# Layer 0 of a four-layer graph kernel: the sigmoid of r is transposed, and multiplied by the transposed x' on its way out of PSUM

## The chip, the cores and the metric

One core of one Trainium2 chip. The metric is the device time of one execution in microseconds. The kernel before was run three times; its median is 3438.73 us.

## The reference

Four layers on x (64 graphs, 256 nodes, 256 features) with adjacency adj (64 x 256 x 256), each followed by a residual sum and a layer norm. Layer 0 is a recurrence over the 256 nodes, and the change is in it alone:

```python
def step(h, i):
    x = jnp.take(h_e, i, axis=1)
    row = jnp.take(norm_adjT, i, axis=1)
    x_par = jnp.einsum('bj,bjd->bd', row, h)
    iou = x @ W_ioux.T + b_ioux + x_par @ W_iouh.T + b_iouh
    r, z = jnp.split(iou, 2, axis=1)
    r, z = (jax.nn.sigmoid(r), jax.nn.sigmoid(z))
    hc = jnp.tanh(x @ W_coux.T + b_coux + x_par * r @ W_couh.T + b_couh)
    h_new = z * x_par + (1.0 - z) * hc
    h = jax.lax.dynamic_update_slice(h, h_new[:, None, :], (0, i, 0))
    return (h, None)
```

Layer 1 is a graph convolution, layer 2 masked attention with one head, layer 3 masked attention with eight heads. All of it is in fp32.

## The kernel before

The kernel first sums, for all graphs, what the nodes not yet updated give to each node's x' (the code's `xp`, the reference's `x_par`). Then `_recurrence` runs 256 unrolled steps n. All 64 graphs are worked on at once: a state tile is 128 x 128, the two halves of the 256 features standing one under the other in the partitions, 64 graphs each. After the recurrence `_layers` runs the other three layers, graph by graph.

The order within the steps is written out by hand: inside the loop a manual schedule is in force, so each engine runs its instructions in the order in which the Python loop issues them, and waits in that order. What must go from one step to the next is a chain:

- x' is transposed by TensorE (`flip`, L611) and copied out of PSUM by ScalarE (L613) as `xpT`.
- `h_part` (L604) multiplies the h weights by it, first for gate r, later for z. Their x products (`x_part`, L596) and the bias are already in PSUM. r and the candidate c share one PSUM tile `rc`.
- ScalarE takes the sigmoid of r in place (L827). VectorE multiplies it by x' as `rx` (L829). `rx` is transposed (L611) and copied (L613) as `rT`, and `h_part` multiplies the candidate's weights by it.
- ScalarE takes the tanh (L861); VectorE makes `zcc` = (1 - z) * c (L863) and the next x' (L866) from it and from `v` (L852), which holds z * x' (`zx`, L843) and what GpSimd made `ready` (L803).
- The new state is added up by VectorE (L645) and copied by ScalarE as `hs` (L647).

Round this chain stands work that the queues fit in:

- `push` (L629) is one VectorE instruction that adds the last state, times an adjacency column, to the sum of one later node. p = n mod 8 decides how many there are: 5 at p = 0, then 10, 9, 8, 7, 6, 6, 4. In the loop they stand in groups: the one that the next node needs; up to 3 before `rx`; 1 after it; up to 4 after `v`. One that does not fit is left to the next step. `push_far` (L662, L666) does up to four more nodes at once on GpSimd.
- Fillers on TensorE: sums over older states (`late`, L520) at p = 0 to 3, `early` products (L417) or those of the x side (L212) at p = 4 to 7, where there are any. The first filler of a step stands behind the transpose of x', the second behind the z products. At p = 0 the second is twice as long, and the transposes of four x tiles (`flip_x`, L577) stand where the first would be; at p = 4 four more of them end the step. Results of fillers are copied out by ScalarE (L255), one or two at a step's middle and one at its end.
- The next step's r and c start with a copy of their bias by ScalarE (L837), then two x products of 256 columns: one between the transpose of `rx` and the c products, one behind the c products.
- Once in some steps VectorE makes degree sums (L303) at a step's end. The late sums travel through DRAM between steps 3 and 5 (L500, L506), and GpSimd adds them after steps 5 and 6 (L875).

The lines of the middle of a step, as they were:

```python
            push(3)
            ...
            h_part(z, 2, xpT)
            ...  # the second filler
            nc.scalar.activation(r, r, AF.Sigmoid)
            rx = new("rx", n, 1)
            nc.vector.tensor_mul(rx, r, xp)
            ...  # 1 - z, z, and the bias of the next rc
            rT = flip(rx, "rT", n)
            push(1)
            zx = keep[:, 2, :]
            nc.vector.tensor_mul(zx, z, xp)
```

Of the kernel before, what the change touches and what calls it, by code (L numbers as in the profile page):

```python
# [9 lines left out]
F32 = mybir.dt.float32  # L10
BF16 = mybir.dt.bfloat16
AF = mybir.ActivationFunctionType
# [7 lines left out]
P = 128  # L20
# [50 lines left out]
def _recurrence(tc, ident, Hd, x, adj, W_ioux, b_ioux, W_iouh, b_iouh, W_coux, b_coux, W_couh, b_couh, wide, then):  # L71
# [19 lines left out]
    nc = tc.nc  # L91
# [12 lines left out]
    with ExitStack() as ctx:  # L104
# [480 lines left out]
        def bias_part(G, gates):  # L585
            for o in range(2):
                nc.tensor.matmul(
                    G[o * B:(o + 1) * B], ones3, bias3[:, o, gates], start=True, stop=False,
                    skip_group_check=True,
                )  # L590

        def x_part(G, n, kc, gates):
            a, u = divmod(n, U)
            h, i = divmod(u, U // 2)
            for o in range(2):
                nc.tensor.matmul(  # L596
                    G[o * B:(o + 1) * B], xqT[a, i // 2][:, i % 2, kc, h * B:(h + 1) * B],
                    WxT[:, kc, o, gates], start=False, stop=False, skip_group_check=True,
                )

        def h_part(G, g, hT):
            for kc in range(2):
                for o in range(2):
                    nc.tensor.matmul(  # L604
                        G[o * B:(o + 1) * B], hT[:, kc * B:(kc + 1) * B], WhT[:, kc, o, g],
                        start=False, stop=(kc == 1), skip_group_check=True,
                    )

        def flip(src, tag, n):
            pt = ps.tile([P, P], F32, tag="flip", name=f"{tag}_ps_{n}")  # L610
            nc.tensor.transpose(pt, src, ident)  # L611
            t = new(tag, n, 1)
            nc.scalar.copy(t, pt)  # L613
            return t

        def new(tag, n, bufs=2):
            return work.tile([P, P], F32, tag=tag, name=f"{tag}_{n}", bufs=bufs)

        def cell(j, m, count=1):

            a, u = divmod(m, U)
            k, i = divmod(m, T)
            return sums[a][:, u:u + count, :], tables[k]["S"][:, LAG + j - k * T, i:i + count]

        def push(count):
            for _ in range(min(count, len(pushes))):
                m, j = pushes.pop(0)
                acc, s = cell(j, m)
                nc.vector.scalar_tensor_tensor(  # L629
                    acc[:, 0, :], keep[:, j % 2, :], s, acc[:, 0, :], ALU.mult, ALU.add  # L630
                )
# [80 lines left out]
        ps = ctx.enter_context(tc.tile_pool(name="r_ps", bufs=1, space=bass.MemoryType.PSUM))  # L712
# [9 lines left out]
        rc = ps.tile([P, 2, P], F32, tag="rc", name="rc_0", bufs=2)  # L722
# [9 lines left out]
        xp = new("xp", 0)  # L732
# [8 lines left out]
        def fill(side, n):  # L741

            try:
                side.send(n)
                return True
            except StopIteration:
                return False

        def fill_early(n):
            nonlocal x_left  # L750
            if not early_fill(n):
                for _ in range(2 if p in (6, 7) else 1):
                    if x_left and not fill(x_left, n):
                        x_left = None

        ctx.enter_context(tc.manual_schedule())
        for now in range(N):
            n = now
            k, i = divmod(n, T)
            p = n % U  # L760
            last = n + 1 == N

            xpT = flip(xp, "xpT", n)
# [25 lines left out]
            r, c = rc[:, 0, :], rc[:, 1, :]  # L789
# [10 lines left out]
            if not last:  # L800
# [3 lines left out]
                    ready, sums[(n + 1) // U][:, (n + 1) % U, :],  # L804
                    dinv[:, n + 1:n + 2].to_broadcast([P, P]),
                )
            push(3)
            if far:
                push_far(n - 1, hs, far[0], len(far))
            if behind:  # L810
# [7 lines left out]
                    early_parts.clear()  # L818
            h_part(z, 2, xpT)

            if p < 4:
                for _ in range(2 if p == 0 else 1):
                    fill(late_side, n) if late_side else None
            else:
                fill_early(n)

            nc.scalar.activation(r, r, AF.Sigmoid)  # L827
            rx = new("rx", n, 1)
            nc.vector.tensor_mul(rx, r, xp)  # L829
            zc = new("zc", n, 1)  # L830
            nc.scalar.activation(zc, z, AF.Sigmoid, scale=-1.0)
            nc.scalar.activation(z, z, AF.Sigmoid)
            if not last:
                rc = ps.tile([P, 2, P], F32, tag="rc", name=f"rc_{n + 1}", bufs=2)
# [2 lines left out]
                    nc.scalar.copy(rc, bias_rc)  # L837
                else:
                    bias_part(rc, slice(0, 2))
            rT = flip(rx, "rT", n)  # L840
            push(1)
            zx = keep[:, 2, :]
            nc.vector.tensor_mul(zx, z, xp)  # L843
            if not last:
                x_part(rc, n + 1, 0, slice(0, 2))
            h_part(c, 1, rT)
            for _ in range(2 if p == 3 else 1):
                next_of(copies, n)
            if not last:
                Sd = tables[kk]["Sd"][:, ii:ii + 1]  # L850
                v = keep[:, 3, :]
                nc.vector.scalar_tensor_tensor(v, zx, Sd, ready, ALU.mult, ALU.add)  # L852
                push(4)
                x_part(rc, n + 1, 1, slice(0, 2))
                z = ps.tile([P, P], F32, tag="z", name=f"z_ps_{n + 1}")
                bias_part(z, 2)
                for kc in range(2):
                    x_part(z, n + 1, kc, 2)
# [5 lines left out]
            if not last:  # L864
                xp = new("xp", n + 1)
# [542 lines left out]
def kernel(ctx: ExitStack, tc: tile.TileContext, ins, out):  # L1408
# [14 lines left out]
    def load_layers(load):  # L1423
        weights.extend(
            _load_layers(nc, wide, load, ins["L1_gnn_W"], ins["L1_gnn_b"], l2, l3)
        )

    _recurrence(
        tc, ident, Hd, x, adj,
        *(ins["L0_gnn_" + n] for n in (  # L1430
# [44 lines left out]
```

## Time and profile before

| what | value |
|---|---|
| median of 3 runs | 3438.73 us (3435.99 to 3442.99) |
| profiled execution, its own time: the span on the page | 3437.6 us |
| recurrence in it, first xpT copy to the last steps | 140.7 to 1525 us |
| TensorE busy, whole span | 3227.2 us (94%) |
| VectorE busy, whole span | 2499.7 us (73%) |
| ScalarE busy, whole span | 1883.7 us (55%) |
| GpSimd busy, whole span | 1873.5 us (55%) |
| pushes (L629) | 1712, 344 ns each |

The page names no time around the span for this execution; its span is taken as its time. PE is TensorE, PEld its weight loads, DVE VectorE, ACT ScalarE, POOL GpSimd, SP the engine that issues most DMAs. A timeline row gives an instruction's start in us from the span's start, its length, engine, line, operation, output and inputs, shapes, how many were merged (a 128 x 256 fp32 product stands as several records), and in brackets how long the engine was idle before it and what ended that. Starts that follow closer than the lengths are instructions that overlap in an engine's pipeline.

### The profile page before, as it was taken

The page shows a single profiled execution, that of the slowest core. Times are in us where ns is not written, and L with a number is a line of the kernel's source. Part 1 is how long each engine was busy: PE and PEld are TensorE (multiplying, and loading weights), DVE is VectorE, ACT ScalarE, POOL GpSimd, SP SyncE. Part 2 cuts the span into 40 slices and gives each one's busy share as a digit, 9 for nine tenths or more (in the row PEclk, how much of TensorE's full clock was granted, in tenths as well). Part 3 has the DMA queues.
Part 4 walks back from the last instruction along what each step waited for, and adds up shares of the span by engine and source line. Part 5 has one row for each costly group of instructions (what it writes and reads, how often), then busy time and mean ns, then how long its engine had stood idle before and what let it go on. Part 6 is the DMA issues. An engine that isn't in the chain of part 4 may idle for free.

```text
span 3437.6 us, 80347 instructions
## 1 busy us (share of the span) xinstructions
PE 3227.2 (94%) x29350; PEld 2321.8 (68%) x29350; DVE 2499.7 (73%) x7061; ACT 1883.7 (55%) x5010; POOL 1873.5 (55%) x2165
## 2 busy tenths in 40 slices
PE   5699999999889998878999999999999999999997
PEld 3555555555455555547888888888888888888885
DVE  3377777766667777755888888888888887888775
ACT  0155555544445554535666666666666666666664
POOL 2376777766657777733444444444444444444443
PEclk8999999999999999988999999999999999999999
DMA  9856576788777575130111111111111111111100
GB/s 280 245 156 150 159 189 154 169 193 204 194 185 175 148 176 153 58 97 22 47 47 47 47 47 47 47 47 47 47 47 47 47 47 47 47 47 47 47 29 19
DMA packets 389348, 347.88 MB, mean 101 GB/s; under 512 B 107357, under 2 KB 355305, under 8 KB 383721
## 3 DMA queue, kind: packets, MB, share of 16 engines
q1 hardware_dynamic: 371256, 325.82, 35.4%
q10 hardware_dynamic: 17696, 16.91, 1.5%
q8 instruction: 234, 3.83, 0.5%
q14 instruction: 162, 1.32, 0.1%
HBM read 224.01 MB, written 99.61 MB: 94 GB/s over the span
## 4 chain that ended last, share of the span: by engine, by line
PE 73%; DMA 7%; DVE 7%; POOL 4%; issue 3%; ACT 3%; SPq 2%; ACTq 0%; DVEq 0%; POOLq 0%
PE mm L996 13%; PE rc L604 5%; PE s L1180 4%; PE rc L596 4%; PE mm_2f L996 3%; PE mm_3v L996 3%; PE mm_t L996 3%; PE mm_3f L996 3%; PE mm_2v L996 3%; PE mm_g L996 3%; PE mm_2s L996 3%; PE mm_2w L996 3%; PE o L1215 3%; PE late L520 3%; DVE ACC L629 3%
## 5 line engine op out<-in xcount | busy, mean ns | idle before, releaser
L629 DVE SCALAR_TENSOR_TENSOR ACC<-keep,S,ACC 128x128 f32<-128x128 f32 x1712 | 504.0, 344 | 186.4 <-ACT hs L647 171.5
L1192 POOL TENSOR_TENSOR p3s<-p 128x256 f32<-128x256 f32 x512 | 387.2, 788 | 369.1 <-ACT p L1190 369.0
L996 PE MATMUL mm<-xT,weights 128*128 128x256 f32 x2048 | 483.9, 385 | 3.2 <-ACT xT L1078 3.2
L996 PEld LDWEIGHTS mm<-xT,weights 128*128 128x128 f32 x2048 | 386.4, 191 | 80.6 <-issue 25.5
L1189 DVE TENSOR_TENSOR p<-s,neg 128x512 f32<-128x512 f32 x512 | 317.5, 682 | 118.2 <-PE s L1180 118.2
L666 POOL TENSOR_TENSOR ACC<-ACC,far 128x384 f32<-128x384 f32 (+1 forms) x313 | 372.7, 1191 | 24.5
L596 PE MATMUL rc<-WxT,xqT 128*64 128x256 f32 x2048 | 324.6, 396 | 3.7 <-ACT rc L837 1.2
L662 POOL TENSOR_TENSOR far<-hs,S 128x384 f32<-128x384 f32 (+1 forms) x313 | 304.9, 974 | 4.7
L960 ACT ACTIVATE y<-y,shift,rstd 128x256 f32<-128x256 f32 x512 | 273.4, 599 | 47.4 <-DVE shift L958 43.4
L1190 ACT ACTIVATE p<-p 128x512 f32<-128x512 f32 x512 | 295.2, 628 | 2.1 <-DVE p L1189 1.6
L803 POOL TENSOR_TENSOR ready<-ACC,dinv 128x128 f32<-128x128 f32 x255 | 102.3, 401 | 335.3 <-DVE ACC L629 335.2
L1103 ACT ACTIVATE qk<-mm,weights 128x256 f32<-128x256 f32 x256 | 107.5, 471 | 268.0 <-PE mm L996 268.0
L1092 POOL TENSOR_TENSOR y<-y,g 128x512 f32<-128x512 f32 x64 | 81.1, 1267 | 267.7 <-issue 267.7
L1229 DVE RECIPROCAL rT<-o 128x256 f32<-128x256 f32 x128 | 223.8, 1748 | 0.3 <-PE o L1206 0.2
L948 DVE BATCH_NORM_STATS2 st<-y 128x6 f32<-128x256 f32 x512 | 209.0, 408 | 13.5 <-POOL y L1092 12.7
L952 POOL TENSOR_TENSOR rstd<-rstd,mhalf 128x2 f32<-128x2 f32 x256 | 173.9, 698 | 82.1 <-DVE rstd L951 80.3
L613 ACT COPY xpT<-xpT_ps 128x128 f32<-128x128 f32 x256 | 68.3, 267 | 259.3 <-PE xpT_ps L611 259.3
L604 PE MATMUL rc<-WhT,xpT 128*64 128x128 f32 x2048 | 170.2, 288 | 29.1 <-ACT xpT L613 28.9
L1057 POOL TENSOR_TENSOR dis<-dis,mhalf 128x2 f32<-128x2 f32 x64 | 44.9, 702 | 276.0 <-DVE dis L1056 265.0
L604 PEld LDWEIGHTS rc<-WhT,xpT 128*64 128x64 f32 x2048 | 107.8, 137 | 120.2 <-ACT xpT L613 84.0
L1155 ACT ACTIVATE qk<-mm,weights 128x256 f32<-128x256 f32 x256 | 107.5, 471 | 118.4 <-PE mm L996 118.4
L596 PE MATMUL z_ps<-WxT,xqT 128*64 128x128 f32 x2048 | 169.7, 287 | 0.0
(162 smaller groups left out, 7418.4 us busy)
## 6 DMA issues: line engine op xcount, KB each, us to landing
xX<-in_x_dram ACTq DMA_DIRECT2D x16, 1024.0 KB
Us<-xu SPq DMA_DIRECT2D x64, 256.0 KB
xq<-in_x_dram SPq DMA_DIRECT2D x64, 256.0 KB
ACC<-Us SPq DMA_DIRECT2D x32, 512.0 KB
Es<-eu SPq DMA_DIRECT2D x64, 256.0 KB
early_sb<-Es SPq DMA_DIRECT2D x32, 512.0 KB
xin<-in_x_dram SPq DMA_DIRECT2D x64, 256.0 KB
ad<-in_adj_dram SPq DMA_DIRECT2D x64, 256.0 KB
```

What stands on the lines that cost most here:

```text
L596: nc.tensor.matmul(G[o * B:(o + 1) * B], xqT[a, i // 2][:, i % 2, kc, h * B:(h + 1) * B], WxT[:, kc, o, gates], start=False, stop=False, s ...
L604: nc.tensor.matmul(G[o * B:(o + 1) * B], hT[:, kc * B:(kc + 1) * B], WhT[:, kc, o, g], start=False, stop=(kc == 1), skip_group_check=True,)
L629: nc.vector.scalar_tensor_tensor(acc[:, 0, :], keep[:, j % 2, :], s, acc[:, 0, :], ALU.mult, ALU.add)
L662: nc.gpsimd.tensor_mul(tmp[:, 0:count, :], hs.unsqueeze(1).to_broadcast(shape), s.unsqueeze(2).to_broadcast(shape),)
L666: nc.gpsimd.tensor_add(acc, acc, tmp[:, 0:count, :])
L948: nc.vector.bn_stats(st, y[:, c, :])
L960: nc.scalar.activation(y[:, c, :], y[:, c, :], AF.Identity, bias=shift[:, c:c + 1], scale=rstd[:, c:c + 1],)
L996: nc.tensor.matmul(pm[:, c, :], lhsT[:, k, c * P:(c + 1) * P], rhs[:, k, :], start=(k == 0), stop=(k == 1),)
L1189: nc.vector.tensor_add(p, s_ps[i], self.neg3)
L1190: nc.scalar.activation(p, p, AF.Exp, scale=ISQ)
L1192: nc.gpsimd.tensor_add(both, p[:, 0, :], p[:, 1, :])
L1229: nc.vector.reciprocal(rT, o_ps[:, 1, :])
```

## The change

The sigmoid of r goes into a new SBUF tile `rs`, which is transposed at once behind the z products. VectorE multiplies the transposed sigmoid, read from PSUM, by `xpT`: the product is `rT`. `rx` and the copy of `rT` are gone. The second filler now stands behind that transpose. Both x products of the next step stand behind the c products. Of the pushes, up to 5 (were 3) stand before the multiply beside the one that the next node needs, none between it and `zx`, and up to 3 (were 4) after `v`.

```diff
-            push(3)
+            push(5)
...
             h_part(z, 2, xpT)
 
+            rs = new("rs", n, 1)
+            nc.scalar.activation(rs, r, AF.Sigmoid)
+            turned = ps.tile([P, P], F32, tag="flip", name=f"rT_ps_{n}")
+            nc.tensor.transpose(turned, rs, ident)
+            rT = new("rT", n, 1)
+            nc.vector.tensor_mul(rT, turned, xpT)
+
             if p < 4:
                 for _ in range(2 if p == 0 else 1):
                     fill(late_side, n) if late_side else None
             else:
                 fill_early(n)
 
-            nc.scalar.activation(r, r, AF.Sigmoid)
-            rx = new("rx", n, 1)
-            nc.vector.tensor_mul(rx, r, xp)
             zc = new("zc", n, 1)
...
-            rT = flip(rx, "rT", n)
-            push(1)
             zx = keep[:, 2, :]
             nc.vector.tensor_mul(zx, z, xp)
-            if not last:
-                x_part(rc, n + 1, 0, slice(0, 2))
             h_part(c, 1, rT)
...
-                push(4)
-                x_part(rc, n + 1, 1, slice(0, 2))
+                push(3)
+                for kc in range(2):
+                    x_part(rc, n + 1, kc, slice(0, 2))
```

## The prediction

> **What bounds the kernel now.** I read the page's slices first, then the recurrence in stretches, then the timeline of single steps, engine by engine, and last the list of waits. The 256 steps run from 140.7 to 1525 us; the rest of the span holds the three other layers, which the change leaves alone.
>
> The page's first line, then two stretches of the recurrence (columns: length, busy time of each engine, clock, DMA share, GB/s):
>
> ```profile
> span 3437.6 us, 80347 instructions
> ```
>
> ```profile
> 476.00:648.00 172.00, 161.23 (x2105) 95.80 (x2107) 124.50 (x429) 90.36 (x312) 124.05 (x135) 1.00 0.66 157
> 648.00:1030.00 382.00, 349.16 (x4473) 199.53 (x4473) 252.13 (x865) 183.05 (x632) 244.16 (x268) 0.95 0.81 194
> ```
>
> TensorE is busy 161.2 of 172.0 us in the undisturbed stretch, so a shorter chain of small operations cannot be cashed in whole. The timeline of one step (n = 65, n mod 8 = 1), TensorE's rows and then VectorE's, and at last two VectorE rows of n = 87 (start, length):
>
> ```profile
> 487.38 0.33 PE L611 MATMUL xpT_ps<-ident,xp 128*128 128x128 f32 x1
> 487.64 0.66 PE L520 MATMUL late<-Hw,An 64*32 64x256 f32 x16
> 488.24 0.66 PE L604 MATMUL rc<-WhT,xpT 128*64 128x128 f32 x8
> 488.72 0.61 PE L604 MATMUL z_ps<-WhT,xpT 128*64 128x128 f32 x8
> 489.26 0.66 PE L520 MATMUL late<-Hw,An 64*32 64x256 f32 x16
> 489.85 0.33 PE L611 MATMUL rT_ps<-ident,rx 128*128 128x128 f32 x1
> 490.16 0.65 PE L596 MATMUL rc<-WxT,xqT 128*64 128x256 f32 x4
> 490.64 0.61 PE L604 MATMUL rc<-WhT,rT 128*64 128x128 f32 x8
> 491.08 0.60 PE L596 MATMUL rc<-WxT,xqT 128*64 128x256 f32 x4
> 491.61 0.24 PE L587 MATMUL z_ps<-bias,ones 3*64 3x128 bf16 x2
> 492.54 0.33 PE L611 MATMUL xpT_ps<-ident,xp 128*128 128x128 f32 x1
> ...
> 488.27 1.13 DVE L629 SCALAR_TENSOR_TENSOR ACC<-keep,S,ACC 128x128 f32<-128x128 f32 x4 [0.67 <-ACT hs L647]
> 489.31 0.28 DVE L829 TENSOR_TENSOR rx<-rc,xp 128x128 f32<-128x128 f32 x1
> 489.51 0.34 DVE L629 SCALAR_TENSOR_TENSOR ACC<-keep,S,ACC 128x128 f32<-128x128 f32 x1
> 489.99 0.30 DVE L843 TENSOR_TENSOR keep<-z_ps,xp 128x128 f32<-128x128 f32 x1
> 490.39 0.36 DVE L852 SCALAR_TENSOR_TENSOR keep<-keep,Sd,ready 128x128 f32<-128x128 f32 x1
> 490.78 1.13 DVE L629 SCALAR_TENSOR_TENSOR ACC<-keep,S,ACC 128x128 f32<-128x128 f32 x4
> 491.83 0.28 DVE L863 TENSOR_TENSOR zcc<-zc,rc 128x128 f32<-128x128 f32 x1
> ...
> 607.62 0.28 DVE L829 TENSOR_TENSOR rx<-rc,xp 128x128 f32<-128x128 f32 x1
> 607.84 0.30 DVE L843 TENSOR_TENSOR keep<-z_ps,xp 128x128 f32<-128x128 f32 x1
> ```
>
> On TensorE one block follows the other; it waits only at the end, before 492.54: in another step the way from the bias product to the next transpose block is 0.76 us (507.61 to 508.37), so 491.61 could have given 492.37, and 0.17 us is waited for xp. VectorE sets that end: tanh is over at 491.56, but zcc starts at 491.83, behind four pushes. So steps with n mod 8 of 1 to 3 (8 to 10 pushes) are set by VectorE's queue at the end; steps 0, 4, 5 and 6 by TensorE's own queue; step 7 (4 pushes) by the chain where it has no filler.
>
> **What the change does to TensorE.** Before, the order behind the z products is filler, transpose, x product, c product, x product. After, it is transpose, filler, c product, two x products: the same blocks. Spacings from the rows above: transpose to filler 0.26 (487.38 to 487.64), filler to the next block 0.60, c product to x product 0.44, x product to bias 0.53, one more x product 0.43. The transpose can start where the filler did (489.26), but waits for the sigmoid, which starts 489.00 and ends 489.26; the hop from a ScalarE end to TensorE is 0.06 (509.81 to 509.87), so 489.32. Filler 489.58, c product possible at 490.17, bias 490.17 + 0.44 + 0.43 + 0.53 = 491.57, against 491.61. TensorE gains 0.04 us a step if nothing is waited for: where TensorE sets the step, the change is worth nothing, and each wait in front of the c product is lost.
>
> **What it does to the chain.** Removed: rx before the transpose (0.28) and the copy of rT (0.27) behind it; added: one multiply out of PSUM. I cost it as rx, 0.28, because rx too reads one PSUM and one SBUF operand. Its earliest start is transpose + 0.33 + 0.09 (490.18 to the rT copy at 490.27) = 489.74. From the sigmoid's end to the c product the chain was 1.38 us (489.26 to 490.64), and is now 0.06 + 0.33 + 0.09 + 0.28 + 0.06 = 0.82. The 0.56 us are hidden nearly everywhere by the two queues.
>
> The sigmoid now writes SBUF where it wrote PSUM. Rows: in place in PSUM 262 ns (L827) and 272 ns (L832), into SBUF 278 ns (L831). That is 6 to 16 ns, on the path in steps 0 and 7 only: 0.4 to 1 us in all, left out of the sum. The Trainium skill ("ScalarE: Activation LUTs", section "Step-by-step: what each stage is for") speaks against this edit: it calls PSUM the faster destination for ScalarE. The rows agree in sign, with a price that decides nothing.
>
> **What it does to VectorE.** Six pushes instead of four stand ahead of the multiply, then the zx product without a push between, and three pushes instead of four before zcc. A push takes 0.26 of the queue (1.04 for four: 488.27 to 489.31).
>
> Steps 1 to 3: multiply at 488.27 + 6 x 0.26 = 489.83, end 490.11, hop 0.06 (492.49 to 492.54): c product 490.17, just when TensorE is ready. How soon zx follows a multiply is the main unknown. Behind a push it comes 0.48 later (489.51 to 489.99), because it waits for that push; behind rx with no push between and its inputs long ready it comes 0.22 later (607.62 to 607.84). After the change a multiply stands directly before it, so I take 0.22 and keep 0.48 as the bad end. zx 490.05, L852 0.40 later at 490.45; from L852 to zcc it was 1.44 with four pushes, 1.18 with three: zcc 491.63 against 491.83. TensorE allows the next transpose at 491.57 + 0.76 = 492.33, VectorE at 492.34. Gain 0.20; the three steps differ by a tenth, so 0.17: 96 x 0.17 = -16.3 us. With 0.48: 0.06 lost, +5.
>
> Step 4 (n = 68): pushes start 504.47, late because a degree sum (0.68 us) stands before them. Six end at 506.03, c product 506.37 against 506.59; bias 506.37 + 1.40 = 507.77 against 507.61, and TensorE sets the rest of this step (four x transposes follow). Loss 0.16: 32 x 0.16 = +5.1 us; bounds 0.05 and 0.25.
>
> Steps 5 and 6: in n = 69 pushes start 510.02, multiply 511.57, c product 511.91. Before, rT was transposed at 511.46 and the first x product began at 511.79; with 0.48 from there, c product 512.27 and bias 513.24; after, 511.91 + 1.40 = 513.31. Loss 0.07, 0.05 over both kinds, with and without filler: 64 x 0.05 = +3.2 us; bounds -0.05 and 0.2.
>
> Step 7 has four pushes in both kernels. Without filler (n = 87): multiply at 607.62 as rx was, c product 607.96 against 608.70; the added x product gives 0.43 back: gain 0.31. With filler 0.11. Mean between them, weighted low since most have filler: 0.15, 32 x 0.15 = -4.8 us; bounds 0.05 and 0.31.
>
> Step 0: a filler twice as long hides all; TensorE sets it before and after: 0, bounds -0.04 and +0.1.
>
> **Moved with it.** The filler's eviction copies on ScalarE follow a filler that ends about 0.3 us earlier against the step's end or the same, so tanh is not held. Nothing moves on GpSimd or on the DMA queues except by time. `ready` (L803) still follows the one push that it needs.
>
> **The disturbed stretch.** From 648 to 1030 us the clock is 0.95, and 65 steps take 382 us where 33 steps take 172 in the stretch before: 43 us more. POOL L875 waits 33.6 us in 12 waits for late_sb, POOL An L478 15.7 us for its raw table. These are transfers, and each long wait is followed by a step at a lower clock that is about 2 us longer. The late sums are sent after step 3 and needed after step 5; step 4 gets 0.16 longer and step 5 0.05, so the wait should shrink by 0.2 us each, 12 times: -2. But the loads are issued by step too, and a shift can open or close a stall with its 2 us; I take 0, from -8 to +10.
>
> **Sum.** -16.3 + 5.1 + 3.2 - 4.8 + 0 = -12.8 us. The profiled execution (span 3437.6) lies 1.1 us under the median of 3438.73; against the median, 3426.
>
> **Rivals.** (a) The pushes ahead of the multiply decide, and the kernel is slower. In six of eight steps the multiply stands behind six pushes; every 0.1 us by which it comes later than reckoned, through a push that waits for GpSimd's sum or through zx at 0.48, costs 192 x 0.1 = 19 us, for TensorE has then no filler left. It decides from a mean delay of 0.07 us on; at 0.1 the time is 3445. For it: no slack at 490.17 and a loss already in steps 4 to 6. Against it: such a push follows without a gap at 489.51. (b) Both queues are conserved and the end of the step moves nowhere, because zx waits 0.48 in steps 1 to 3 while a few stalls close: 3439. For it: TensorE's 0.04. Against it: the 0.22 row. (c) The chain is the bound and its 0.56 us show where fillers do not cover them: TensorE is idle for some 74 us of the recurrence outside the disturbed stretch (1384.3 us less 1277.7 busy, less 33 in that stretch); if half of it went, 3402. For it: the step-7 sum. Against it: rows in which TensorE's next block starts without a gap. (d) The change does not do what it says: each engine runs the loop's program order, so the transpose does stand before the filler; I give this nothing.
>
> **How the numbers follow.** Forecast 0.56, (a) 0.22, (b) 0.14, (c) 0.08. Bounds of the sum: zx at 0.48 alone gives +8, the good ends of steps 5 to 7 and of the stalls about -26. Range 3410 to 3446. A comparison here can tell about 0.2%, 7 us. Faster by more than that: the forecast's larger part and (c), 0.60; within: (b) and the edge of the forecast, 0.16; slower: (a) and the edge of (b), 0.24.
>
> **What would show it.** In the timeline of a step 1, the transpose of rs some 0.6 us after the z products begin, the c product near 2.4 us after the xpT copy starts (2.84 before), zx 0.22 behind the multiply, and zcc 0.2 earlier. A step 4 that is longer by 0.1 to 0.2, a step 7 shorter. I am wrong if the c product waits for the multiply by more than 0.1 us in most steps, if zx keeps 0.48, or if the stretch from 648 to 1030 us changes by more than 10 us.

## The result and the profile after

The changed kernel takes 3439.56 us (median of 12 runs, 3432.54 to 3442.75) against 3441.61 us of the kernel before beside it: ratio 0.999, interval 0.998 to 1.000. On a second chip (e7 below) it was 3434.01 against 3441.99: 0.998, 0.9967 to 0.9993. So it gains 2 to 8 us where 12.8 were forecast. Both intervals leave out the forecast's ratio, 0.9963 (3426 to 3438.73), the second narrowly, and the first just reaches no gain at all.

The page's first line, and the same two stretches of the recurrence (length, busy time of PE, PEld, DVE, ACT, POOL, clock, DMA share, GB/s):

```profile
span 3431.9 us, 79587 instructions
```

```profile
476.00:648.00 172.00, 161.42 (x2119) 98.84 (x2117) 121.96 (x429) 83.51 (x281) 122.34 (x135) 1.00 0.66 157
648.00:1030.00 382.00, 341.60 (x4454) 201.51 (x4450) 246.10 (x861) 169.74 (x567) 243.48 (x267) 0.95 0.80 193
```

In the first stretch TensorE is as busy as before (161.42, before 161.23). In the second, the clock is the same (0.95), and so are DMA share and GB/s (0.80 and 193, before 0.81 and 194), while TensorE was busy 7.6 us less.

The timeline of step n = 65, TensorE's rows, then VectorE's:

```profile
486.82 0.33 PE L611 MATMUL xpT_ps<-ident,xp 128*128 128x128 f32 x1
487.08 0.66 PE L520 MATMUL late<-Hw,An 64*32 64x256 f32 x16
487.67 0.66 PE L604 MATMUL rc<-WhT,xpT 128*64 128x128 f32 x8
488.16 0.61 PE L604 MATMUL z_ps<-WhT,xpT 128*64 128x128 f32 x8
488.77 0.33 PE L824 MATMUL rT_ps<-ident,rs 128*128 128x128 f32 x1
489.03 0.66 PE L520 MATMUL late<-Hw,An 64*32 64x256 f32 x16
489.62 0.66 PE L604 MATMUL rc<-WhT,rT 128*64 128x128 f32 x8
490.11 1.03 PE L596 MATMUL rc<-WxT,xqT 128*64 128x256 f32 x8
491.07 0.24 PE L587 MATMUL z_ps<-bias,ones 3*64 3x128 bf16 x2
...
491.83 0.33 PE L611 MATMUL xpT_ps<-ident,xp 128*128 128x128 f32 x1
...
487.65 1.64 DVE L629 SCALAR_TENSOR_TENSOR ACC<-keep,S,ACC 128x128 f32<-128x128 f32 x6 [0.99 <-ACT hs L647]
489.21 0.28 DVE L826 TENSOR_TENSOR rT<-rT_ps,xpT 128x128 f32<-128x128 f32 x1
489.41 0.29 DVE L845 TENSOR_TENSOR keep<-z_ps,xp 128x128 f32<-128x128 f32 x1
...
490.98 0.28 DVE L864 TENSOR_TENSOR zcc<-zc,rc 128x128 f32<-128x128 f32 x1
```

Step 1 went as reckoned: `zx` follows the multiply by 0.20 (489.21 to 489.41), `zcc` comes early, and TensorE's last wait is gone: from one xpT transpose to the next 5.01 us, end to end without a wait (5.16 before).

Step times read from the starts of the xpT copies (L613), medians over the 24 steps of each kind outside steps 96 to 159, and two sums; two profiles of each kernel:

| n mod 8 | 0 | 1 | 2 | 3 | 4 | 5 | 6 | 7 | steps 96-159 | all others |
|---|---|---|---|---|---|---|---|---|---|---|
| before | 5.31 | 5.16 | 5.16 | 5.47 | 5.77 | 4.88 | 4.96 | 4.96 | 376.4 | 1005.5 |
| before again (e13) | 5.31 | 5.16 | 5.16 | 5.47 | 5.77 | 4.88 | 4.96 | 5.25 | 385.9 | 1009.8 |
| after | 5.45 | 5.01 | 5.01 | 5.01 | 5.99 | 4.95 | 4.95 | 4.82 | 378.3 | 1004.7 |
| after again (e7) | 5.45 | 5.01 | 5.01 | 5.01 | 5.99 | 4.95 | 4.95 | 4.82 | 375.7 | 1006.1 |

By the medians, the usual step gains 0.48 us in eight steps against the first row, 11.5 us in the 24 groups outside 96 to 159. A median is not a mean here: before the change, step 3 takes 5.28 us in some groups and 5.5 to 5.7 in others, and step 7 takes 4.9 or 5.25 and more. What counts are the sums in the last column, on average 1007.6 us before and 1005.4 after: a gain of 2.2 us. The rest must be found in single long steps. Steps 96 to 159 gain nothing that stands out of their own spread: two profiles of the same kernel before are 9.5 us apart there.

### The profile page after: what moved, and what is told of

Same layout as the page of the kernel before. It is cut to its first block, busy times and chain, and to the rows that moved or that the text cites. A ratio compares the mean times of both kernels' runs of the same rounds, so it can differ in the third digit from the quotient of the medians.

```text
span 3431.9 us, 79587 instructions
## 1 busy us (share of the span) xinstructions
PE 3219.7 (94%) x29350; PEld 2339.7 (68%) x29350; DVE 2480.2 (72%) x7061; ACT 1827.7 (53%) x4754; POOL 1871.0 (55%) x2165
## 4 chain that ended last, share of the span: by engine, by line
PE 73%; DMA 9%; DVE 6%; SPq 3%; POOL 3%; issue 3%; ACT 2%; ACTq 0%; POOLq 0%; DVEq 0%
PE mm L997 13%; PE rc L604 5%; PE rc L596 4%; PE s L1181 4%; PE mm_2f L997 3%; DVE ACC L629 3%; PE mm_3v L997 3%; PE mm_t L997 3%; PE mm_3f L997 3%; PE mm_2v L997 3%; PE mm_g L997 3%; PE mm_2s L997 3%; PE mm_2w L997 3%; PE o L1216 3%; PE late L520 3%
## 5 line engine op out<-in xcount | busy, mean ns | idle before, releaser
L629 DVE SCALAR_TENSOR_TENSOR ACC<-keep,S,ACC 128x128 f32<-128x128 f32 x1712 | 481.3, 344 | 256.5 <-ACT hs L647 228.1
L596 PE MATMUL rc<-WxT,xqT 128*64 128x256 f32 x2048 | 268.1, 382 | 0.6 <-issue 0.6
L1104 ACT ACTIVATE qk<-mm,weights 128x256 f32<-128x256 f32 x256 | 107.3, 470 | 269.6 <-PE mm L997 269.6
L613 ACT COPY xpT<-xpT_ps 128x128 f32<-128x128 f32 x256 | 68.1, 266 | 302.5 <-PE xpT_ps L611 302.5
L604 PE MATMUL rc<-WhT,rT 128*64 128x128 f32 x2048 | 170.2, 287 | 58.0 <-DVE rT L826 56.0
L604 PEld LDWEIGHTS rc<-WhT,rT 128*64 128x64 f32 x2048 | 107.8, 137 | 158.1 <-DVE rT L826 137.0
```

Source lines behind the costliest of these rows:

```text
L596: nc.tensor.matmul(G[o * B:(o + 1) * B], xqT[a, i // 2][:, i % 2, kc, h * B:(h + 1) * B], WxT[:, kc, o, gates], start=False, stop=False, s ...
L604: nc.tensor.matmul(G[o * B:(o + 1) * B], hT[:, kc * B:(kc + 1) * B], WhT[:, kc, o, g], start=False, stop=(kc == 1), skip_group_check=True,)
L629: nc.vector.scalar_tensor_tensor(acc[:, 0, :], keep[:, j % 2, :], s, acc[:, 0, :], ALU.mult, ALU.add)
```

## Experiments

Ratios are to the kernel before in the same session, with their intervals; "outside" means steps outside 96 to 159.

**The wait for the late sums taken away, in both kernels (e1, e2).**

```diff
-                nc.gpsimd.tensor_add(part, part, sides[n + 8 - p][:, half])
+                nc.gpsimd.tensor_add(part, part, nothing.unsqueeze(2).to_broadcast([P, U // 2, P]))
```

> The kernel before, but the add of L875 (POOL, into the sums of the next steps) reads a tile of zeros instead of late_sb: the late sums are left out of the result, all other work stays. Theory A (the step got shorter, and the transfers of the late sums give the time back): the 33.6 us of waits and the clock steps behind them go, so this kernel loses 30 to 45 us against the kernel before, to about 3400; and the pair of this run and the next differs by 10 to 15 us. Rival B (the waits are not what eats the gain): the same loss here or less, but the pair differs by 0 to 4 us.

> The changed kernel with the same cut: the add of the late sums reads zeros, so the late sums are left out of the result. Theory A: 40 to 60 us below the changed kernel (its waits were 43.8 us), about 3387, 10 to 15 us below the run before. Rival B (the change's own steps 0 and 4 give back what steps 1 to 3 gain): 0 to 4 us below the run before; steps 1 to 3 shorter by 0.2, steps 0 and 4 longer by as much as without the cut.

Measured: 3470.04 us (1.0083, 1.007 to 1.0096) and 3450.06 us (1.0034, 1.0023 to 1.0046). Both became slower, by 31 and 11 us, so my sizes for both were wrong in sign. Steps 96 to 159 take 383.4 and 380.6. The list of waits of e2 shows where the wait went:

```profile
PE late L520 <- DMA Hw<-hs: 22.3, 6, 6.6
PE late L520 <- DMA A<-in_adj_dram: 14.4, 3, 9.5
```

TensorE itself now waits for other transfers, in step 0. In the changed kernel these waits are 0.4 and 1.6 us. In e1 the first of them is 18.7 us, in the kernel before it does not occur. So with the add's wait gone its time was not saved. The pair differs by 20 us in the change's favour.

**The late sums' transfers taken away, in both kernels (e5, e6).** As e1 and e2, and besides:

```diff
-            def then(n):
-                at_step(n, send)
-                at_step(n + 1, receive)
...
-                                then if g and u + 2 == NG // 2 else None,
+                                None,
```

> The kernel before without the late sums' way through DRAM: no stores to Lb, no load of late_sb, and the add of L875 reads zeros, so the late sums are left out of the result. Theory A2 (transfers, not one wait, pace steps 96 to 159: these took 376.4, 383.4, 378.3, 380.6, 377.9 and 382.6 us in six kernels whose other steps differ by up to 46): about 1 MB less in 8 steps, so steps 96 to 159 take clearly less than 376, 350 to 365; the kernel is 10 to 40 us faster than before. Rival (the stretch is paced by the adjacency loads and the order of their issue alone): 370 to 383 again.

> The changed kernel with the same cut (late sums left out of the result). Theory A2: faster than the run before by 10 to 20 us, because the shorter steps 1 to 3 and 7 now count in all 32 blocks of 8 steps and no push waits for the late sums; steps with n mod 8 = 6 at 4.95. Rival B (the change gains little in its own steps): 0 to 5 us.

Measured: 3433.74 us (0.9974, 0.9962 to 0.9986) and 3422.16 us (0.9945, 0.9927 to 0.9963). Steps 96 to 159 shrink to 361.0 and 356.5, and this is the only edit of all that shortens them. From 648 to 1030 us 174 and 180 GB/s are moved instead of 194 and 193; whether the bytes, the number of transfers or their order count isn't separated. The granted clock over these steps rose (0.97 and 0.98, before 0.95), but it doesn't set the stretch: in e14 below it is 0.98 too, and they take 384.5. e5 gains 8 us, less than the 10 to 40 expected, in part because its other steps take 1017.9, 8 to 12 more than before. The pair differs by 11.6 us, near the forecast's 12.8, and neither has a stall at step 25.

**Step 25, and two orders of step 0 (e7, e8, e3).** e7 is the changed kernel again. e8 and e3 move one or both pieces of step 0's filler ahead of the transpose, and leave one or none behind it:

```diff
+            if p == 0 and late_side:
+                fill(late_side, n)          # e8: once; e3: twice, ahead of the sigmoid
             turned = ps.tile([P, P], F32, tag="flip", name=f"rT_ps_{n}")
```

> The changed kernel once more, beside the others on this chip. Theory: the stall of 5.4 us at step 25 (and 1.9 in the next) belongs to the changed order, then it stands here again and the recurrence takes about 1383; rival: it is chance of one execution, then it is gone, steps outside 96 to 159 take 997 to 1000 instead of 1004.7. In both, steps with n mod 8 = 6 have a multiply that comes 0.6 to 9 us late in some six to ten of 32 blocks, behind the sixth push.

> The changed kernel, but in steps with n mod 8 = 0 one of the two pieces of filler stands ahead of the transpose and one behind it. Theory: the wait for the sigmoid and the filler's semaphore waits are then worked off behind running products; the c product starts 2.75 after the xpT copy instead of 2.88, the step takes 5.30 to 5.35 instead of 5.45, as before the change: -3 to -4 us. Rival: the step is lost to the second piece whatever stands before it; 5.45 again, or more if the transpose comes too late (5.67 with both pieces ahead).

> The changed kernel, but in steps with n mod 8 = 0 the two pieces of filler stand ahead of the sigmoid and the transpose again. Theory B: the filler's semaphore waits (four of about 0.105 us on TensorE's queue) are again worked off while the products run; step 0 gets back 0.15 to 0.27 us, 32 times: -5 to -9 us, so about 3432. Rival: step 0's loss is the multiply out of PSUM or the six pushes, then step 0 stays at 5.45 and the time within 2 us of the changed kernel. Theory A: step 0 shorter, but the time within 2 us, given to the transfers.

e7: step 25 takes 10.44 us in both profiles, 5.4 too much, and step 26 another 1.9 too much, at a granted clock of 0.69 and 0.68 (before: 1.00). That is 7.3 us in both profiles of the changed kernel and in neither of the kernel before. TensorE's rows in the first profile, and the DMA view of the gap (272.2 to 277.1 us):

```profile
271.32 1.03 PE L596 MATMUL rc<-WxT,xqT 128*64 128x256 f32 x8
277.03 0.32 PE L587 MATMUL z_ps<-bias,ones 3*64 3x128 bf16 x2 [4.68 <-issue]
```

```profile
DMA packets 325, 0.03 MB, mean 7 GB/s; under 512 B 324, under 2 KB 324, under 8 KB 324
...
q8 instruction: 1, 0.02, 1.2%
```

"issue" says that TensorE waited for nothing that the profile shows. But one packet of the instruction queue (16 KB) begins in the gap, at 274.85 us, and TensorE goes on 2.2 us later; in e7 the packet begins at 276.26 and TensorE goes on 2.2 us later too. Where this gap is shorter, the distance is the same: in e2, e4 and e16 TensorE goes on 2.2 to 2.3 us after the packet begins. I read it as a block of instructions that came late.

e8: 3433.50 us (0.9982, 0.997 to 0.9994); step 0 at 5.38. e3: 3433.07 us (0.9985, 0.9975 to 0.9995); step 0 at 5.67. In both, step 25 is at 5.01. But e8 is no faster than e7 beside it (3434.01), though it lacks the stall: the totals do not confirm the 7.3 us, which stand in the profiles alone. For step 0, e3's expectation fell: with all filler in front, the c product waits for the multiply, 3.09 after the xpT copy instead of 2.88. One piece in front (e8) gives back half of the 0.14 lost in the usual step 0. But in six others (n = 16, 32, 40, 56, 64 and 72) that piece takes 1.14 instead of 0.59 us and the step 5.9, for a reason that stays open, so the mean over the 24 steps is 5.54 against 5.50 and nothing is gained. The rows of n = 64 show the loss, first in the changed kernel, then before:

```profile
483.04 0.33 PE L824 MATMUL rT_ps<-ident,rs 128*128 128x128 f32 x1
483.46 1.22 PE L520 MATMUL late<-Hw,An 64*32 64x256 f32 x32
484.61 0.66 PE L604 MATMUL rc<-WhT,rT 128*64 128x128 f32 x8
```

```profile
483.84 1.09 PE L520 MATMUL late<-Hw,An 64*32 64x256 f32 x32
484.87 0.33 PE L611 MATMUL rT_ps<-ident,rx 128*128 128x128 f32 x1
```

The double filler starts 0.42 behind the transpose, not 0.26: that 0.16 is the loss of the usual step 0. TensorE's queue has four semaphore instructions ahead of this filler, 0.105 us apart in the trace. Before, they started 0.39 to 0.71 after the xpT copy, while products ran; now they start at 1.42 to 1.74, with the transpose that waits for the sigmoid, and the filler's first product follows at 1.85. In n = 64 a fifth one delays the filler's second product, and its successor comes 1.15 later (483.46 to 484.61) where 1.03 is usual and was so before (483.84 to 484.87): this is one of the same six steps, which take 5.57.

**What made the block late (e12, e15).**

```diff
-                if i in (0, 2, 3, 8, 10, 11, 12, 15, 16, 17, 19, 20, 22, 24):
+                if i in (0, 2, 3, 8, 10, 11, 12, 15, 16, 17, 19, 20, 22, 26):   # e12
-            if i == 24:
-                flush(n - 8 - T, n - 8)
+            if i == 22:                                                         # e15
+                flush(n - 6 - T, n - 6)
```

> The changed kernel, with dinv's four stores (L237, issued for 10 to 11 us from SP) two steps later, at n mod 32 = 26. Theory (the 4.7 us in which TensorE stood in step 25, in both profiles of the changed kernel, were a block of instructions that arrived behind dinv's transfers): step 25 at 5.0 to 5.1 and step 26 at 5.0 or a little more, -6 to -7 us, about 3428. Rival (the gap belongs to the place in the program): 10.4 us again. Third: the gap moves to another instruction two steps on.

> The changed kernel with the flush of Hw to Hd (L637) two steps earlier, at n mod 32 = 22, the same rows. Theory (the block of instructions that step 25 waits for stands behind the flush): step 25 at 5.0 to 5.2, -7 us in the recurrence, or the gap moves ahead by some steps if the block is then asked for behind another transfer. Rival (the place in the program alone): 10.2 to 10.4 us again.

e12: 3434.28 us (0.9985, 0.9973 to 0.9997), step 25 at 10.17: `dinv`'s stores are not the cause. e15: step 25 at 5.01, but 3463.26 us (1.0058, 1.0044 to 1.0072), since seven steps, six with n mod 8 = 0 and step 55, now take 11 to 18 us. So the gap goes when the flush moves, but the kernel's whole traffic moved with it. The same program on TensorE has no such gap when only VectorE's order differs (e4: step 25 at 5.70; e16: 5.92). I read this as a place that belongs to the program and a length that the transfers of that moment set; that is not shown, and which of them delays the block stays open.

**The pushes (e4, e16, e11).**

```diff
-            push(5)                          # ahead of the multiply
+            push(3 if 4 <= p <= 6 else 5)    # e4;  e16: push(4 if p == 6 else 5);  e11: push(3)
...
-                push(3)                      # ahead of zcc
+                push(5 if 4 <= p <= 6 else 3)  # e4;  e16: push(4 if p == 6 else 3);  e11: push(5)
```

> The changed kernel, with the split of the pushes by step: in steps 4 to 6 three ahead of the multiply and five ahead of zcc, elsewhere five and three as in the changed kernel. Theory B: step 4's multiply comes 0.5 us earlier, step 4 goes from 5.77 to about 5.6 and steps 5 and 6 lose 0.05 to 0.1: 32 x 0.17 + 64 x 0.07 = -10 us, about 3430. Rival: zcc, now behind five pushes, sets the end of steps 5 and 6, which get 0.1 to 0.3 longer: +2 to +14. Theory A: steps shorter, the time within 2 us.

> The changed kernel with four instead of five pushes ahead of the multiply in steps with n mod 8 = 6 (four and four): the push into the sums that L876 adds to then stands behind the multiply. Theory (the wait is conserved, because transfers pace steps 96 to 159): no multiply late by 0.6 to 9 us in these steps, 2 us less outside 96 to 159, these at 376 to 382 again: within 3 us of the changed kernel. Rival (the sixth push's wait of 22.7 us is the cost): -10 to -20 us.

> The changed kernel with three pushes ahead of the multiply and five ahead of zcc in all steps. Theory (in steps 1 to 3 VectorE sets the end, and the gain there is the pushes moved ahead of the multiply): zcc at about 4.1 instead of 3.80 after the xpT copy, steps 1 to 3 at 5.25 to 5.40 instead of 5.01, +18 to +28 us over 72 steps, steps 4 to 6 as with the split by step, -12: 3440 to 3452. Rival (TensorE sets these steps whatever VectorE does): 5.01 again, and about 3425.

e4: 3426.54 us (0.9957, 0.9944 to 0.997). Steps 4, 5, 6 at 5.52, 4.76, 4.95; outside 986.2, of which 7 us are the gap that is absent. Six pushes ahead of the multiply were what step 4 lost.

e16: 3432.24 us (0.9962, 0.995 to 0.9974). In step 6 the sixth push writes into the sums to which L876 adds the late sums. In the changed kernel, step 94 (VectorE):

```profile
641.04 1.38 DVE L629 SCALAR_TENSOR_TENSOR ACC<-keep,S,ACC 128x128 f32<-128x128 f32 x5 [0.99 <-ACT hs L647]
643.68 0.35 DVE L629 SCALAR_TENSOR_TENSOR ACC<-keep,S,ACC 128x128 f32<-128x128 f32 x1 [1.25 <-POOL ACC L876]
643.94 0.28 DVE L826 TENSOR_TENSOR rT<-rT_ps,xpT 128x128 f32<-128x128 f32 x1
```

Five pushes run, the sixth waits 1.25 us for GpSimd, and the multiply stands behind it. Waits of the changed kernel, then of e16:

```profile
PE rc L604 <- DVE rT L826: 55.8, 81, 9.2
POOL ACC L876 <- DMA late_sb<-Lb: 43.8, 12, 13.2
DVE ACC L629 <- POOL ACC L876: 22.7, 10, 9.2
DVE keep L852 <- POOL ready L803: 13.2, 2, 10.6
```

```profile
PE rc L604 <- DVE rT L826: 32.5, 75, 0.9
POOL ACC L876 <- DMA late_sb<-Lb: 47.5, 11, 12.5
DVE keep L852 <- POOL ready L803: 36.5, 10, 8.6
DVE ACC L629 <- POOL ACC L876: 11.2, 8, 1.4
```

The first row is TensorE's wait for the multiply in front of the c product (total in us, times, longest). With four pushes ahead it shrinks by 23 us, while VectorE's waits for GpSimd change their place and don't shrink: 22.7 + 13.2 became 11.2 + 36.5. Steps 96 to 159 take 379.6. Outside, step 6 gains 4 us and step 25's gap is short, but step 0 loses 5 (mean 5.73); e16 is 0.0018 to 0.0028 better than the changed kernel (6 to 10 us) in ratios from different chips, more than the 3 us expected, and how much of that is step 6 and how much the gap isn't separated.

e11: 3436.11 us (0.9987, 0.9976 to 0.9999). Steps 1 and 2 go to 5.32, step 3 to 5.45: VectorE sets their end, as reckoned. The total is below the expectation, 7 us of it because step 25's gap is absent in the profile.

**The parts alone (e10, e14).** e10 has the new arithmetic behind the second filler, with the x products and pushes of the kernel before:

```diff
-            nc.scalar.activation(r, r, AF.Sigmoid)
-            rx = new("rx", n, 1)
-            nc.vector.tensor_mul(rx, r, xp)
+            rs = new("rs", n, 1)
+            nc.scalar.activation(rs, r, AF.Sigmoid)
+            turned = ps.tile([P, P], F32, tag="flip", name=f"rT_ps_{n}")
+            nc.tensor.transpose(turned, rs, ident)
+            rT = new("rT", n, 1)
+            nc.vector.tensor_mul(rT, turned, xpT)
...
-            rT = flip(rx, "rT", n)
```

e14 has the old arithmetic in the new order: sigmoid, `rx`, transpose and rT copy stand ahead of the second filler.

```diff
             h_part(z, 2, xpT)
 
+            nc.scalar.activation(r, r, AF.Sigmoid)
+            rx = new("rx", n, 1)
+            nc.vector.tensor_mul(rx, r, xp)
+            rT = flip(rx, "rT", n)
...
-            if not last:
-                x_part(rc, n + 1, 0, slice(0, 2))
             h_part(c, 1, rT)
...
-                x_part(rc, n + 1, 1, slice(0, 2))
+                for kc in range(2):
+                    x_part(rc, n + 1, kc, slice(0, 2))
```

> The changed arithmetic alone: sigmoid into SBUF, transpose, multiply out of PSUM, with filler, x products and pushes (three, one, four) where they were before the change. Theory: rx and the copy of rT lay beside other work, so steps 1 to 3 stay at 5.16, steps 0 and 4 at 5.31 and 5.77, step 7 gains up to 0.2; 3433 to 3441. Rival (the shorter chain is itself the gain): steps 1 to 3 at 5.0, 3425 or less.

> The kernel before with the reordering alone: rx, transpose and rT copy as before, but the transpose ahead of the filler, both x products behind the c product, pushes as before. Theory: rx ends 0.35 us after the sigmoid, behind four pushes, so the transpose waits for VectorE and TensorE stands ahead of the filler 0.3 to 0.5 us in each step, with no other block to fill it: steps 0 to 6 longer by 0.2 to 0.4, +40 to +80 us. Rival (the order is worth more than the arithmetic): within 10 us of before.

e10: 3506.44 us (1.0188, 1.017 to 1.0207), 65 us slower. I had expected no loss. VectorE's rows of step 65, and TensorE's last:

```profile
505.38 1.12 DVE L629 SCALAR_TENSOR_TENSOR ACC<-keep,S,ACC 128x128 f32<-128x128 f32 x4 [0.56 <-ACT hs L647]
507.39 0.29 DVE L832 TENSOR_TENSOR rT<-rT_ps,xpT 128x128 f32<-128x128 f32 x1 [0.88 <-PE rT_ps L830]
507.60 0.34 DVE L629 SCALAR_TENSOR_TENSOR ACC<-keep,S,ACC 128x128 f32<-128x128 f32 x1
508.04 0.30 DVE L845 TENSOR_TENSOR keep<-z_ps,xp 128x128 f32<-128x128 f32 x1
...
510.60 0.33 PE L611 MATMUL xpT_ps<-ident,xp 128*128 128x128 f32 x1 [0.99 <-DVE xp L868]
```

The multiply waits on VectorE for a transpose that stands behind the filler, and a push, `zx`, `v`, four pushes and `zcc` stand behind the multiply. The 0.88 us come out again as TensorE's wait of 0.99 at the end: 6.05 in steps 1 and 2.

e14: 3555.25 us (1.0326, 1.031 to 1.0342), 110 us slower, beyond the 40 to 80 expected. TensorE's, ScalarE's and VectorE's rows of step 65:

```profile
525.52 0.33 PE L611 MATMUL rT_ps<-ident,rx 128*128 128x128 f32 x1 [0.32 <-DVE rx L823]
...
525.88 0.27 ACT L613 COPY rT<-rT_ps 128x128 f32<-128x128 f32 x1 [0.76 <-PE rT_ps L611]
...
526.22 0.29 ACT L834 ACTIVATE z_ps<-z_ps 128x128 f32<-128x128 f32 x1
...
526.53 0.30 DVE L844 TENSOR_TENSOR keep<-z_ps,xp 128x128 f32<-128x128 f32 x1 [0.81 <-PE late L520]
```

The transpose waits 0.32 for `rx`, as expected. What I missed is the copy of rT: in this order it stands ahead of z's sigmoid (L834) on ScalarE, and `zx` starts 0.03 after that sigmoid's end, 2.86 after the xpT copy instead of 2.18. (The bracket of `zx` names the filler, whose last product started at 526.07.) So each half alone costs 65 or 110 us, and both together, with the pushes of e11, gain 5.

Steps 96 to 159 take 382.7 in e10 and 384.5 in e14, though their other steps are 0.33 and 0.56 us longer on average, some 21 and 36 us over 64 steps: longer steps, too, left hardly a mark on this stretch, which takes 376.4 and 385.9 in the two profiles of before.

**Before again, and the best version (e13, e9).** e9 has e4's split of the pushes, also in step 7, and e8's filler.

```diff
-            push(5)
+            push(3 if p > 3 else 5)
...
-                push(3)
+                push(5 if p > 3 else 3)
```

> The kernel before once more, for a second profile. Theory: recurrence 1380 to 1384, steps 96 to 159 at 374 to 380, the others at 1003 to 1007, first xpT copy at 139 to 142 (the changed kernel: 136.5 and 137.8). Rival: the first profile's setup was slow by chance and the second begins at 137, then nothing of the measured difference lies in the setup.

> The changed kernel with three pushes ahead of the multiply and five ahead of zcc in steps with n mod 8 over 3 (five and three elsewhere), and in step 0 one piece of filler ahead of the transpose. Theory (the sums of steps add up outside 96 to 159): steps 4 to 6 at 5.55, 4.75 and 4.85 instead of 5.99, 4.95 and 4.95, step 0 at 5.38 instead of 5.45, step 7 at 4.8 to 4.9: -6 - 4 - 3 - 2 = -15 us, and -7 more if the gap at step 25 is gone with the new order of TensorE's instructions: 3415 to 3424. Rival (five pushes ahead of zcc cost step 7 what the others gain): 3430.

e13: 0.9998 (0.9985 to 1.0011). Its setup ended at 138.7 us, between the first profile's 140.7 and the changed kernel's 136.5 and 137.8: no difference there can be claimed. Its steps 96 to 159 took 385.9 us, its profiled execution 3449.57 as a whole. Of the 10.1 us between the spans of these two profiles, the stretch makes 9.5.

e9: 3421.46 us (0.9947, 0.9933 to 0.9962), faster than both kernels and as expected. Steps 0, 4, 5, 6 at 5.38, 5.52, 4.76, 4.95; step 25 at 5.01; outside 985.4; steps 96 to 159 at 381.7. Step 7 went to 5.03 instead of 4.8 to 4.9, perhaps because pushes that were held back are due there. Against e4 (0.9957, outside 986.2) e8's filler adds nothing that can be told.

## Why the prediction was wrong

The step that failed is the term for stalls, which I put at 0 and looked for only from 648 to 1030 us. In the profiles a stall at step 25 cost 7.3 us outside that stretch. What the change does within the steps came out as reckoned. Means over the steps outside 96 to 159, without the excess of steps 25 and 26, two profiles of each kernel, us per step:

| n mod 8 | 0 | 1 | 2 | 3 | 4 | 5 | 6 | 7 |
|---|---|---|---|---|---|---|---|---|
| reckoned | 0 | -0.17 | -0.17 | -0.17 | +0.16 | +0.05 | +0.05 | -0.15 |
| measured | +0.09 | -0.16 | -0.16 | -0.25 | +0.15 | +0.05 | +0.09 | -0.21 |

- The price of `zx`, the main unknown, was right: 0.20 against 0.22. In steps 1 to 3 the c product starts 2.43 after the xpT copy (2.4 reckoned) and waits for the multiply by more than 0.1 us in 8 of 96 steps. TensorE's wait for the multiply, 55.8 us in 81 waits in the whole recurrence, lies mostly in other steps, most often in step 4 (29 of 32).
- The sigmoid into SBUF: 277 ns (L822) against 262 ns in place in PSUM (L827). So the Trainium skill's advice in "ScalarE: Activation LUTs" (section "Step-by-step: what each stage is for") that PSUM is the faster destination for ScalarE agrees with this trace, with 15 ns, too little to decide anything here.
- **Step 0**, reckoned at 0 with bounds up to +0.1, was +0.14 in the usual step: 24 times 3.4 us. (The mean above is smaller because the second profile of before has one step 0 that is 3.4 us too long.) I hid the transpose behind the filler, but not the filler's semaphore waits behind the transpose.
- **"The disturbed stretch: 0"** fits the number: 376.4 and 385.9 us before, 378.3 and 375.7 after. But the step terms were counted over all 32 groups of eight, and eight of them, 3.2 of the 12.8 us, lie in steps 96 to 159. I had no ground to count them: neither steps 0.3 to 0.6 us longer (e10, e14) nor the shorter steps of e4 and e9 moved that stretch out of 376 to 386 us, while removing transfers did. Whether 3.2 us came out there can't be read from a stretch that varies by 10.
- **Step 25** cost 7.3 us in both profiles of the changed kernel and about as much in e12, and no row of before could show it. The bound of +10 that I gave the stalls covers it in size, but it lies outside the disturbed stretch. No part of the change aims at it, so whether a kernel has it is luck as far as these runs show, and its cause stays open.

Together, outside 96 to 159: the forecast's terms for these steps make -9.6 us (24 of 32 groups), the sums of the steps without the stall -9.5, and with its 7.3 us -2.2. The two comparisons have -2 and -8, with the stretch's own spread of several us in each. So the shortfall is accounted for in the profiled executions; the total of e8, which lacks the stall, is not lower by it, so how much of it every execution pays isn't shown.

One sum in the range is off: with the good ends of steps 5 to 7 and of the stalls, the terms make about -32, not -26. Nothing hangs on it.

Of the rivals, (b) named the time, 3439, by the wrong way and so by luck: `zx` did not wait. (a) found the push that waits for GpSimd's sum, but only in step 6, and e16 shows that VectorE's wait there mostly moves to another place. (c) fell.

## What to carry to other kernels

Before multiplying a gain per step by the number of steps, take out the steps that something else paces: here a stretch with a DMA share of 0.8 kept its length in every order of the steps, and a wait taken away came back at another consumer. Compare sums of steps besides medians: the median hid step 3's two lengths before and six slow steps in e8. When an operation goes to another engine, look at what stands behind it in that engine's order: here each half of the change alone cost 65 or 110 us, since the multiply or the copy then stood waiting ahead of `zx`. And split fixed counts, such as these pushes, by the kind of step: e4 took 0.9957 of the time of before, the change alone 0.998 to 0.999.

## What the runs showed of the hardware

- Taking away a wait on GpSimd (33.6 us) made the kernel 31 us slower (e1): TensorE then waited itself for transfers, 18.7 us for one tile alone.
- In six profiles of the same TensorE program (after, e2, e4, e7, e12, e16), TensorE stood at the same place until 2.2 to 2.3 us after a 16 KB packet began on the instruction queue: for 4.4 to 4.7 us in three of them, for 0.6 to 0.8 us in the others. In e11 and e15 it stood there for less.
- Semaphore instructions in TensorE's queue follow each other by 0.105 us. Four of them cost nothing while products ran (before), and 0.16 us behind a transpose that waited for the sigmoid (after, step 0).
